# A graph network on one core: other association of the products, transposes laid on the host, and the stages of two pairs alternating

## The chip, the cores and the metric

The kernel runs on one core of a Trainium2 chip, all in float32. The metric is the device time of one launch in microseconds (us). The profile names the engines PE (TensorE matmul), PEld (TensorE weight load), DVE (VectorE), ACT (ScalarE), POOL (GpSimd) and SP (the queue that issues the loads).

## The reference, cut to what matters

There are 64 graphs of N = 256 nodes with D = 512 features, and a dense adjacency of 256 x 256 each.

```python
# layer 0: three graph convolutions, each  adj @ (h @ W) + b
h = relu(adj @ (x @ W1) + b1)
h = relu(adj @ (h @ W2) + b2)
x = layernorm(x + adj @ (h @ W3) + b3)
# layer 1: one weight per node, softmax over a graph's nodes
q, k = split(x @ Wqk, 2); v = x @ Wv
w = mask / sqrt(D) * rowsum(q * (adj @ (mask * k)))
x = layernorm(x + softmax(w)[:, None] * v)
```

## The kernel before: the parts that matter here

It works on 32 pairs of graphs. A layer is made as (adj @ h) @ W: the aggregation comes out transposed, features on partitions, and so serves as the stationary operand of the projection. The scores are rowsum((x1 @ M) * (adj @ (mask * x1))) with M = Wq @ Wk.T.

```python
def transpose_adj(i, aj, k):                       # 4 TensorE transposes a graph
    pt = psum.tile([P, NH, N], FP, name="pa", tag="mm")
    for m in range(NH):
        for h in range(NH):
            nc.tensor.transpose(pt[:, m, h * P:(h + 1) * P], aj[:, k, h, m * P:(m + 1) * P], ident)
    aT = work.tile([P, NH, N], FP, name="aT", bufs=4)
    nc.scalar.copy(aT, pt)
    ...                                            # aTm = aT * mask, on GpSimd

# aggregate(h, aT):     16 products of 128x256 per pair  -> pz
# project(srcT, w, h):  16 products of 128x512 per pair  -> pp

for i in range(NP + 1):
    ...
    aTs = [transpose_adj(i, aj, k) for k in ks]
    if last is not None:
        sm = softmax_rows(last[2])
    zs = [aggregate(xt[:, k], aTs[k][0]) for k in ks]
    ...
    if last is not None:                           # layer 1's end, one pair late
        s = softmax_cols(sm)
        for k in ks:
            layer1_out(i - 1, k, last[0][k], last[1][k], s)
    for n in range(2):
        hs = [hidden(zs[k], n) for k in ks]        # VectorE adds the bias, ScalarE does Relu
        zs = [aggregate(hs[k], aTs[k][0]) for k in ks]
    x1s = [layer0_out(zs[k], xt[:, k]) for k in ks]
    x1Ts = [scores(i, k, x1s[k], aTs[k][1], w) for k in ks]
```

Of the kernel before, what the change touches and what calls it, by code (L numbers as in the profile page):

```python
# [13 lines left out]


@with_exitstack
def gcn_then_graph_attention(ctx: ExitStack, tc: tile.TileContext, x, adj, nodemask,
                             W1, b1, W2, b2, W3, b3, Wqk, Wv, out):
    """Layer 0: x1 = LN(x + GCN3(x)), each GCN layer as (adj @ h) @ W + b.
    Layer 1: x2 = LN(x1 + softmax_i(w) * (x1 @ Wv)), with  # L20
    w = mask / sqrt(D) * rowsum((x1 @ (Wq @ Wk.T)) * (adj @ (mask * x1))).

    adj @ h is made transposed (features on partitions), which is the form that
    the product with W takes as its stationary operand; that product comes out
    with nodes on partitions again. Two graphs go side by side, so that the
    tensor engine has one's products while the other's are brought out of PSUM.
    """
    nc = tc.nc
    P = 128
    B, N, D = x.shape  # L30
    NH = N // P
    DC = D // P
    PAIR = 2
# [5 lines left out]
    work = ctx.enter_context(tc.tile_pool(name="work", bufs=2))  # L39
# [4 lines left out]
    def load_pair(i):  # L44
        bs = slice(i * PAIR, (i + 1) * PAIR)
        aj = loads.tile([P, PAIR, NH, N], FP, name="aj")
        nc.sync.dma_start(aj, adj[bs].rearrange("b (h p) m -> p b h m", p=P))
        xt = loads.tile([P, PAIR, NH, D], FP, name="xt")
        nc.sync.dma_start(xt, x[bs].rearrange("b (h p) f -> p b h f", p=P))  # L49
        return xt, aj  # L50
# [6 lines left out]
    loaded = load_pair(0)  # L57

    mask_n = const.tile([B, N], FP, name="mask_n")
    nc.sync.dma_start(mask_n, nodemask)  # L60

    def load_w(w, name):
        t = const.tile([P, DC, D], FP, name=name)
        nc.sync.dma_start(t, w.rearrange("(c p) h -> p c h", p=P))
        return t

    def load_b(b, name):
        t = const.tile([P, D], FP, name=name)
        nc.sync.dma_start(t, b.partition_broadcast(P))
        return t  # L70

    wl, bl = [], []
    for n, (w, b) in enumerate(((W1, b1), (W2, b2), (W3, b3))):
        wl.append(load_w(w, f"w{n}"))
        bl.append(load_b(b, f"b{n}"))
    wqk_rows = []
    for f in range(DC):
        t = work.tile([P, 2 * D], FP, name="wqk", tag="x1", bufs=4)
        nc.sync.dma_start(t, Wqk[f * P:(f + 1) * P, :])
        wqk_rows.append(t)  # L80
    wv = load_w(Wv, "wv")

    mask_t = const.tile([P, NH, B], FP, name="mask_t")
    mask_s = const.tile([P, NH, B], FP, name="mask_s")
    pm = psum_s.tile([P, NH, B], FP, name="pm", tag="sm")
    for h in range(NH):
        nc.tensor.transpose(pm[:, h, :], mask_n[:, h * P:(h + 1) * P], ident[:B, :B])
    nc.vector.tensor_copy(mask_t, pm)
    nc.vector.tensor_scalar(mask_s, mask_t, ISCALE, None, op0=OP.mult)

    m_qk = const.tile([P, DC, D], FP, name="m_qk")

    def make_m():
        """m_qk = Wq @ Wk.T"""
        halves = []
        for s in range(2):
            for dp in range(DC // 2):
                t = work.tile([P, 2, D], FP, name="wqkT", tag="x1T", bufs=4)
                for k in range(2):
                    c = s * D + (2 * dp + k) * P  # L100
                    pt = psum.tile([P, D], FP, name="pt", tag="mm")
                    for f in range(DC):
                        nc.tensor.transpose(pt[:, f * P:(f + 1) * P], wqk_rows[f][:, c:c + P], ident)  # L103
                    if k:
                        nc.vector.tensor_copy(t[:, k, :], pt)
                    else:
                        nc.scalar.copy(t[:, k, :], pt)
                halves.append(t)
        qT, kT = halves[:DC // 2], halves[DC // 2:]
        for f in range(DC):  # L110
            pt = psum.tile([P, D], FP, name="pt", tag="mm")
            for d in range(DC):
                nc.tensor.matmul(pt, lhsT=qT[d // 2][:, d % 2, f * P:(f + 1) * P], rhs=kT[d // 2][:, d % 2, :],  # L113
                                 start=(d == 0), stop=(d == DC - 1))
            nc.scalar.copy(m_qk[:, f, :], pt)

    def transpose_adj(i, aj, k):
        pt = psum.tile([P, NH, N], FP, name="pa", tag="mm")
        for m in range(NH):
            for h in range(NH):  # L120
                nc.tensor.transpose(pt[:, m, h * P:(h + 1) * P], aj[:, k, h, m * P:(m + 1) * P], ident)  # L121
        aT = work.tile([P, NH, N], FP, name="aT", bufs=4)
        nc.scalar.copy(aT, pt)  # L123
        aTm = work.tile([P, NH, N], FP, name="aTm", bufs=4)
        b = i * PAIR + k
        for m in range(NH):
            nc.gpsimd.tensor_scalar(aTm[:, m, :], aT[:, m, :], mask_t[:, m, b:b + 1], None, op0=OP.mult)  # L127
        return aT, aTm

    def aggregate(h_in, aT):  # L130
        """(adj @ h).T, features on partitions"""
        zT = work.tile([P, DC, N], FP, name="zT", bufs=3)
        for fp in range(DC // 2):
            pz = psum.tile([P, 2, N], FP, name="pz", tag="mm")
            for j in range(2):
                f = 2 * fp + j
                for m in range(NH):
                    nc.tensor.matmul(pz[:, j, :], lhsT=h_in[:, m, f * P:(f + 1) * P], rhs=aT[:, m, :],  # L138
                                     start=(m == 0), stop=(m == NH - 1))
            if fp % 2:  # L140
                nc.vector.tensor_copy(zT[:, 2 * fp:2 * fp + 2, :], pz)  # L141
            else:
                nc.scalar.copy(zT[:, 2 * fp:2 * fp + 2, :], pz)  # L143
        return zT

    def project(srcT, w, h):
        """rows of half h of src @ w, from src transposed"""
        pp = psum.tile([P, D], FP, name="pp", tag="mm")
        for f in range(DC):
            nc.tensor.matmul(pp, lhsT=srcT[:, f, h * P:(h + 1) * P], rhs=w[:, f, :],  # L150
                             start=(f == 0), stop=(f == DC - 1))
        return pp

    def hidden(zT, n):
        hn = work.tile([P, NH, D], FP, name="hn", bufs=3)
        for h in range(NH):
            pp = project(zT, wl[n], h)
            t = work.tile([P, D], FP, name="t", bufs=3)
            nc.vector.tensor_tensor(t, pp, bl[n], op=OP.add)  # L159
            nc.scalar.activation(hn[:, h, :], t, AF.Relu)  # L160
        return hn

    def layernorm(dst, src):
        st = small.tile([P, NH, 6], FP, name="st")
        mv = small.tile([P, NH, 2], FP, name="mv")
        for h in range(NH):
            nc.vector.bn_stats(st[:, h, :], src[:, h, :])  # L167
            nc.vector.bn_aggr(mv[:, h, :], st[:, h, :])  # L168
        sd = small.tile([P, NH], FP, name="sd")
        nc.scalar.activation(sd, mv[:, :, 1], AF.Sqrt, bias=eps)  # L170
        rs = small.tile([P, NH], FP, name="rs")
        nc.vector.reciprocal(rs, sd)
        for h in range(NH):
            nc.vector.tensor_scalar(dst[:, h, :], src[:, h, :], mv[:, h, 0:1], rs[:, h:h + 1],  # L174
                                    op0=OP.subtract, op1=OP.mult)

    def layer0_out(zT, xb):
        r = work.tile([P, NH, D], FP, name="r", bufs=2)
        for h in range(NH):
            pp = project(zT, wl[2], h)  # L180
            nc.vector.tensor_tensor(r[:, h, :], pp, xb[:, h, :], op=OP.add)  # L181
        x1 = work.tile([P, NH, D], FP, name="x1", bufs=4)
        layernorm(x1, r)
        return x1

    def transpose_x1(x1):
        x1T = work.tile([P, DC, N], FP, name="x1T", bufs=4)
        for fp in range(DC // 2):
            pt = psum.tile([P, 2, N], FP, name="px", tag="mm")
            for j in range(2):  # L190
                f = 2 * fp + j
                for h in range(NH):
                    nc.tensor.transpose(pt[:, j, h * P:(h + 1) * P], x1[:, h, f * P:(f + 1) * P], ident)  # L193
# [26 lines left out]
    def softmax_rows(w):  # L220
        """softmax over the nodes, one graph per partition"""
        pw = psum_s.tile([PAIR, N], FP, name="pw", tag="sm")
        for h in range(NH):
            nc.tensor.transpose(pw[:, h * P:(h + 1) * P], w[:, h, :], ident)  # L224
# [32 lines left out]
    for i in range(NP + 1):  # L257
# [16 lines left out]
        if i == NP:  # L274
            break
# [32 lines left out]
```

## Time and profile before

| | before |
|---|---|
| time, median of 2 runs | 3232.23 us |
| span of the profiled run | 3230.6 us |
| TensorE busy | 3215.3 us (100%) |
| VectorE, ScalarE, GpSimd busy | 32%, 17%, 9% |
| TensorE starts / last product ends | 8.12 / 3223.4 us |
| one pair in mid-run | 99.85 us |
| granted TensorE clock | 0.999 |

The chain of work that ended last is followed back from the last instruction, each step to what released it. TensorE has it from 8.12 us until the last product. What comes after is short. These are the last pieces of that chain in order of time (start, length in us, what; a bare "issue" is time in which nothing that the profile shows was waited for):

```profile
3213.79 9.65 PE pp L150 x22
...
3223.47 0.76 DVE r L248
3224.25 0.70 DVE st L167
...
3226.28 0.46 DVEq L304
```

Only 7.2 us follow the last product (3223.44 to 3230.6): VectorE needs few instructions for the last half graph, and the output is written graph by graph. One more line belongs here, from the groups of waits (engine and what it was about to do, on whom it waited, us in total, times, longest):

```profile
PEld pz L138 <- ACT aT L123: 5.6, 31, 0.2
```

Once in each pair, the weight load of the first aggregation waits for the copy of the transposed adjacency.

### The profile page before, as it was taken

The numbers are of one execution on the slowest core, as the hardware profiler recorded it, in microseconds if no ns is written. First come the engines' busy times: TensorE is split into PE (matmuls) and PEld (weight loads), VectorE is DVE, ScalarE is ACT, GpSimd is POOL, SyncE is SP. The second block draws the span as 40 slices with busy tenths as digits, with TensorE's granted clock in tenths as the row PEclk, the third lists the DMA queues.
The fourth block names the chain that finished last, engine by engine and source line by source line (L and its number), as shares of the span: only waits on it lengthen the run. The fifth ranks groups of instructions, "written<-read, shape, count | busy, mean of one in ns | idle before, by whom it ended". The sixth has DMA issues, their size and how long they took to land.

```text
span 3230.6 us, 23926 instructions
## 1 busy us (share of the span) xinstructions
PE 3215.3 (100%) x9666; PEld 1753.3 (54%) x9666; DVE 1033.9 (32%) x2055; ACT 561.7 (17%) x970; POOL 276.0 (9%) x262
## 2 busy tenths in 40 slices
PE   8999999999999999999999999999999999999999
PEld 5555555555555555555555555555555555555554
DVE  1332323323333233233332332323323333333233
ACT  2111111111111111111111111111111111111111
POOL 1110011110111101111001110011110111101110
PEclk9999999999999999999999999999999999999999
DMA  3110001000000000010000000001000001000000
GB/s 134 33 33 20 26 20 33 33 20 26 20 33 33 20 26 21 32 33 26 26 27 20 33 30 23 26 20 33 33 20 26 20 33 33 20 26 20 26 14 13
DMA packets 54509, 92.55 MB, mean 29 GB/s; under 512 B 2240, under 2 KB 18688, under 8 KB 54400
## 3 DMA queue, kind: packets, MB, share of 16 engines
q1 hardware_dynamic: 54400, 91.04, 8.3%
q8 instruction: 76, 1.25, 0.2%
q14 instruction: 33, 0.27, 0.0%
HBM read 57.48 MB, written 33.55 MB: 28 GB/s over the span
## 4 chain that ended last, share of the span: by engine, by line
PE 100%; DMA 0%; DVE 0%; SPq 0%; DVEq 0%; issue 0%; ACT 0%
PE pp L150 68%; PE pz L138 21%; PE pg L208 7%; PE px L193 2%; PE pa L121 1%; PE pt L113 0%; PE pw L224 0%; PE ps L239 0%; DMA mask_n<-in_nodemask 0%; PE pt L103 0%; DVE r L248 0%; DVE st L167 0%; DVE o L174 0%; SPq L49 0%; DVEq L304 0%
## 5 line engine op out<-in xcount | busy, mean ns | idle before, releaser
L150 PE MATMUL pp<-w,zT 128*128 128x512 f32 x3072 | 1334.0, 592 | 0.0
L150 PEld LDWEIGHTS pp<-w,zT 128*128 128x128 f32 x3072 | 583.7, 190 | 707.4 <-issue 704.1
L138 PE MATMUL pz<-aT,hn 128*128 128x256 f32 x2048 | 452.5, 379 | 0.0
L150 PE MATMUL pp<-m_qk,x1T 128*128 128x512 f32 x1024 | 449.9, 592 | 0.0
L150 PE MATMUL pp<-wv,x1T 128*128 128x512 f32 x1024 | 448.3, 595 | 0.0
L138 PEld LDWEIGHTS pz<-aT,hn 128*128 128x128 f32 x2048 | 389.1, 190 | 80.2 <-issue 30.6
L159 DVE TENSOR_TENSOR t<-pp,b 128x512 f32<-128x512 f32 x256 | 177.1, 692 | 626.5 <-PE pp L150 626.5
L127 POOL TENSOR_SCALAR aTm<-aT,mask_t 128x256 f32<-128x256 f32 x128 | 117.0, 932 | 2817.8 <-ACT aT L123 2817.8
L150 PEld LDWEIGHTS pp<-m_qk,x1T 128*128 128x128 f32 x1024 | 194.6, 190 | 244.9 <-issue 244.9
L150 PEld LDWEIGHTS pp<-wv,x1T 128*128 128x128 f32 x1024 | 191.8, 190 | 229.5 <-issue 229.0
L160 ACT ACTIVATE hn<-t 128x512 f32<-128x512 f32 x256 | 161.3, 630 | 782.0 <-DVE t L159 782.0
L141 DVE COPY zT<-pz 128x512 f32<-128x512 f32 x192 | 132.9, 692 | 470.2 <-PE pz L138 470.2
L216 DVE SCALAR_TENSOR_TENSOR prod<-pp,mask_s,g 128x512 f32<-128x512 f32 x128 | 96.1, 751 | 499.2 <-PE pp L150 499.2
L138 PE MATMUL pz<-aT,xt 128*128 128x256 f32 x1024 | 231.3, 384 | 0.0
L208 PE MATMUL pg<-x,aTm 128*128 128x512 f32 x512 | 230.3, 592 | 0.0
L138 PEld LDWEIGHTS pz<-aT,xt 128*128 128x128 f32 x1024 | 193.2, 191 | 31.0 <-ACT aT L123 5.6
L170 ACT ACTIVATE sd<-mv,eps 128x2 f32<-128x2 f32 x128 | 37.9, 296 | 836.8 <-DVE mv L168 836.8
L167 DVE BATCH_NORM_STATS2 st<-r 128x6 f32<-128x512 f32 x256 | 177.5, 693 | 7.7
L248 DVE SCALAR_TENSOR_TENSOR r<-pp,s,x 128x512 f32<-128x512 f32 x128 | 96.1, 751 | 219.4 <-PE pp L150 219.4
L143 ACT COPY zT<-pz 128x512 f32<-128x512 f32 x192 | 111.6, 581 | 296.2 <-PE pz L138 296.2
L269 POOL TENSOR_TENSOR xt<-xt,b 128x512 f32<-128x512 f32 x128 | 159.3, 1264 | 25.1 <-PE pz L138 20.4
L181 DVE TENSOR_TENSOR r<-pp,xt 128x512 f32<-128x512 f32 x128 | 88.5, 692 | 227.5 <-PE pp L150 218.9
(45 smaller groups left out, 893.2 us busy)
## 6 DMA issues: line engine op xcount, KB each, us to landing
xt<-in_x SPq DMA_DIRECT2D x32, 1024.0 KB, 5.4
out<-o SPq DMA_DIRECT2D x64, 512.0 KB, 2.8
aj<-in_adj SPq DMA_DIRECT2D x32, 512.0 KB, 3.8
w<-in_L_gnn_W SPq DMA_DIRECT2D x3, 1024.0 KB, 10.6
wqk<-in_L_gnn_Wqk SPq DMA_DIRECT2D x4, 512.0 KB, 11.9
wv<-in_L_gnn_Wv SPq DMA_DIRECT2D x1, 1024.0 KB, 12.3
b<-in_L_gnn_b SPq DMA_DIRECT2D x3, 256.0 KB, 11.1
mask_n<-in_nodemask SPq DMA_DIRECT2D x1, 64.0 KB, 6.2
```

What stands on the lines that cost most here:

```text
L127: nc.gpsimd.tensor_scalar(aTm[:, m, :], aT[:, m, :], mask_t[:, m, b:b + 1], None, op0=OP.mult)
L138: nc.tensor.matmul(pz[:, j, :], lhsT=h_in[:, m, f * P:(f + 1) * P], rhs=aT[:, m, :], start=(m == 0), stop=(m == NH - 1))
L141: nc.vector.tensor_copy(zT[:, 2 * fp:2 * fp + 2, :], pz)
L143: nc.scalar.copy(zT[:, 2 * fp:2 * fp + 2, :], pz)
L150: nc.tensor.matmul(pp, lhsT=srcT[:, f, h * P:(h + 1) * P], rhs=w[:, f, :], start=(f == 0), stop=(f == DC - 1))
L159: nc.vector.tensor_tensor(t, pp, bl[n], op=OP.add)
L160: nc.scalar.activation(hn[:, h, :], t, AF.Relu)
L167: nc.vector.bn_stats(st[:, h, :], src[:, h, :])
L208: nc.tensor.matmul(pg, lhsT=aTm[:, m, h * P:(h + 1) * P], rhs=x1[:, m, :], start=(m == 0), stop=(m == NH - 1))
L216: nc.vector.scalar_tensor_tensor(prod, py, mask_s[:, h, b:b + 1], gs[h], op0=OP.mult, op1=OP.mult, accum_out=w[:, h, k:k + 1])
L248: nc.vector.scalar_tensor_tensor(r[:, h, :], pv, s[:, h, k:k + 1], x1[:, h, :], op0=OP.mult, op1=OP.add)
L269: nc.gpsimd.tensor_tensor(xt[:, k, h, :], xt[:, k, h, :], bl[2], op=OP.add)
```

## The change

Its intent is to take all transposes but that of x1 off TensorE, to fold the hidden layers' biases into the eviction, and to keep TensorE supplied by giving it another pair's stage between any two stages of one pair. A layer becomes adj @ (h @ W), the scores become masked-adj * (y @ x1.T) with y = x1 @ M, and x and adj come in twice, natural and transposed by the host. The core of the diff (loads, weight layouts and signature are cut):

```diff
-        aT = work.tile([P, NH, N], FP, name="aT", bufs=4)
-        nc.scalar.copy(aT, pt)                        # and the transposes into pt
+    def load_aT(i):
+        t = loads.tile([P, G, NH, N], FP, name="aT", bufs=3)
+        nc.sync.dma_start(t, adjT[i])
 ...
-            t = work.tile([P, D], FP, name="t", bufs=3)
-            nc.vector.tensor_tensor(t, pp, bl[n], op=OP.add)
-            nc.scalar.activation(hn[:, h, :], t, AF.Relu)
+            nc.scalar.activation(hT[:, f], pz, AF.Relu, bias=bias[:, f:f + 1])
 ...
-            pg = psum.tile([P, D], FP, name="pg", tag="mm")         # adj @ (mask x1), 128x512
-            py = project(x1T, m_qk, h)                              # x1 @ M
+            pg = psum.tile([P, NH, N], FP, name="pg", tag="mm")     # y @ x1.T, 128x256
+            for h in range(NH):
+                for d in range(DC):
+                    nc.tensor.matmul(pg[:, h, :], lhsT=yT[:, d, g, h * P:(h + 1) * P], rhs=x1T[:, d, g, :],
+                                     start=(d == 0), stop=(d == DC - 1))
 ...
+    for i in range(NP + 1):
+        new = i < NP
+        if new:              s = project(x0, w1, "s", 2)
+        if prev is not None: layer0_out(prev, aTs[i - 1], xt)
+        if new:              hT = aggregate_relu(s, aTs[i], bl1)
+        if prev is not None: x1T = transpose_x1(xt)
+        if new:              s = project(hT, w2, "s", 2)
+        if prev is not None: yT = project_T(x1T, wm)
+        if new:              hT = aggregate_relu(s, aTs[i], bl2)
+        if prev is not None: w = scores(i - 1, yT, x1T, an)
+        if new:              s = project(hT, w3, "s", 2)
+        if prev is not None:
+            sm = softmax_rows(w)
+            v = project(x1T, wv, "vs", 1)
+            layer1_out(i - 1, xt, v, softmax_cols(sm))
```

## The prediction

> **What bounds the kernel now.** I read first the page's busy time by engine, then its chain of work that ended last, then the same chain in order of time over one pair of graphs in mid-run, and last the groups of waits.
>
> ```profile
> PE 3215.3 (100%) x9666; PEld 1753.3 (54%) x9666; DVE 1033.9 (32%) x2055; ACT 561.7 (17%) x970; POOL 276.0 (9%) x262
> ...
> PE 100%; DMA 0%; DVE 0%; SPq 0%; DVEq 0%; issue 0%; ACT 0%
> ```
>
> TensorE is busy for 3215.3 of 3230.6 us, and the chain is TensorE from beginning to end: no eviction, no load and no semaphore is on it except at the two ends. A busy TensorE could still be a stretched one, so I look at one period of the chain, from one start of a layer-1 projection to the next (1055.46 to 1155.31, 99.85 us for a pair):
>
> ```profile
> 1055.46 13.73 PE pp L150 x32
> 1069.19 6.91 PE pz L138 x32
> 1076.10 13.73 PE pp L150 x32
> 1089.83 0.87 PE px L193 x8
> ...
> 1112.18 0.88 PE pa L121 x8
> 1113.06 0.30 PE pw L224 x2
> 1113.36 7.16 PE pz L138 x32
> 1120.52 0.21 PE ps L239 x2
> 1120.73 27.66 PE pp L150 x64
> 1148.40 6.91 PE pz L138 x32
> ```
>
> The columns are start, length, what. One program matmul of 128x512 leaves two records; 32 records last 13.73 us, so such a matmul costs 0.858 us, one of 128x256 0.432 us (6.91 / 16), a 128x128 transpose 0.109 us (0.87 / 8). These are start-to-start rates, not the longer means of the page's groups, which contain the drain.
>
> **What the Trainium skill says.** "FP8 and Floating Point Precision", section TensorE Precision Notes, gives true FP32 four passes through the array. "TensorE: Matmul & The Clock Gate", section Back-to-back issue gap, gives 518 cycles for one pass of 512 columns at 2.4 GHz, 0.216 us. Four make 0.863 us; this trace has 0.858, so it agrees, and the two kernels cannot differ in rate as long as the type stays. "PSUM — Partial Sum Buffer", section The four PSUM rules, limits one matmul output to one 2 KiB bank, so the seven general buffers of either kernel hold seven stages' outputs of 128x512 in flight. "DMA: Bandwidth & Descriptors", section Anatomy of one DMA, fits about 2.0 us plus bytes over 436 GB/s for a transfer on another issuing path; here 1 MB of x takes 5.4 us (median of 32), somewhat slower than that fit's 4.4.
>
> **The change part by part.** TensorE first, since only it matters. Counting the loops per pair before: three layers of 16 projections, 8 for adj @ x1, 16 with m_qk and 16 with Wv make 88 matmuls of width 512; three aggregations of 16 make 48 of width 256; 8 adjacency and 16 x1 transposes. After: 3 x 16 projections, 8 for the third layer's adj @ s, 16 for y = x1 @ M and 16 with Wv: again 88. Two aggregations of 16 and 16 for y @ x1.T: again 48. So associating the product the other way, and taking the scores from y @ x1.T, **trades equal for equal**: an N x N product over D costs what the removed third aggregation cost. What goes is the transposing.
> - Removed per pair: 8 transposes, 0.88 us; over 32 pairs 28 us. Also the first aggregation's wait for their copy: it took 7.16 instead of 6.91 us, about 0.2 us each, and the groups of waits agree: weight loads of pz waited for the copy to aT 31 times, up to 0.2 us. That is 6 to 8 us. At start-up, 32 transposes of Wqk (3.7 us) and two of the mask (0.4 us). Sum: **38 to 40 us removed**, 1.2% of the time, all of it on the path.
> - Removed elsewhere: bias additions as separate VectorE work (256 x 692 ns = 177 us) become part of the Relu eviction; copies of the transposed adjacency (34.5 us of ScalarE) and its masking. VectorE had 68% idle, ScalarE 83%: this is worth nothing. Plain copies of the projections (8 a pair with Wv's) come in; estimated from rows of the page, VectorE's work per pair is 14 copies or adds at 0.69, 8 statistics at 0.69 and 8 aggregations at 0.18, 8 normalizations at 0.54, 4 scale-and-adds at 0.75, 4 products over 256 columns at about 0.45: some 27 us in a period of 99.
> - Added traffic: x and adj come twice, once transposed: about 4.3 MB a pair with the output, against 2.5, so 43 GB/s where start-up shows 370 to 410 in stretches of 2 to 4 us. The issue order has each load of a pair almost one period ahead. Hidden.
> - Moved: the third layer's end and all of layer 1 of pair i-1 now lie between the stages of pair i. In the built order each consumer in TensorE's queue has a whole stage of the other pair before it. The tightest is normalization: with layer-0 output starting at 0, its products end at 6.9 and the aggregation of the other pair at 13.7; VectorE needs add 0.69, statistics 0.69 + 0.18, square root 0.36 with its semaphore, reciprocal 0.17, two normalizations 1.1 after the last product, so about 10.7 with one Relu before the square root. Then 3 us of slack. The stages of the fill (pair 0 alone) need the last eviction, about 0.97 us after the last product, only after three 0.43 us matmuls of other operands: no stall either.
> So a full iteration is five stages of 13.73 (W1, W2, W3, M, Wv), two aggregations of 6.91, 6.87 for layer 0's output, 6.91 for scores, 1.75 for transposes and 0.51 for the small ones: 98.5. I take 98.65 for small interruptions.
> - Start: the first matmul now needs x transposed and all of W1, 2 MB. Before, 1.56 MB had landed at 7.98 us (the wait for the mask, at the chain's head); at 380 GB/s another 0.5 MB is 1.3 us: TensorE starts at about 9.3 instead of 8.1. The first few microseconds ran slower before as well (first pz stage 8.72 for 7.16): 1.7 us.
> - **End**: the last pair has no partner. From the end of the previous pair's Wv: VectorE finishes that pair's output (about 8.9 us of work), then adds and normalizes the last pair; its rows in the built order sum to 18.9 us until the second graph is normalized; a transpose and a copy later, at about 20.2, y can begin. TensorE has 8.6 us of work in that time, so 11 to 12 us are idle. Then 13.73 + 6.91 + 13.73 + 0.8 of products: 55.4. Then copies, scale-and-add and normalization of four half-graphs, 9.6 us, and a 1 MB write of about 5.5 us (0.5 MB took 3.9 to the end of the span before): 70.5, and 1.7 for a slower restart. Of 72 us TensorE works 44; so 28 idle against 7.2 after the last product before: **21 us added**.
>
> Sum from below: 9.3 + 1.7 + fill 68.7 (four stages of 13.73, two of 6.91) + 31 x 98.65 = 3058.2 + 72.2 gives a span of 3210.1; the timed run was 1.6 longer than the span: 3211.7. By differences: 3232.2 - 39 + 1.2 + 21 = 3215.4. I take 3213.
>
> **The rivals.**
> - The alternation stalls each pair: single buffers for hT, x1T, yT and the projected values could make TensorE wait. For it: the pools are shallower, and VectorE does layer 1's output beside the next projection. Against: every writer of those follows its last reader by a stage of 7 to 14 us, and a buffer of PSUM is asked back seven allocations later. Missing by 2 us would give about 3275; it takes 2.7 us a period to be slower by 2%.
> - The end costs less, because the scheduler's rows overlap better or the write is hidden: 3200. Or more, with the span near 3222.
> - A larger win, as the intent suggests: no adjacency transposes, biases inside the evictions, TensorE never waiting. Against: TensorE's remaining products alone are 2832 x 0.858 + 1536 x 0.432 + 512 x 0.109 + 16 = 3166 us; a gain over 2% would need 3168. All but impossible.
> - Loads in the loop arriving late (xT has a single buffer). Its load can go out when the first projection ends, 85 us ahead: no.
>
> **Range and chances.** The removal is sure within 3 us, the end within 8, the period within 0.3 (9 us over 31). Range 3203 to 3226. Faster by over 2%: 0.01. Within 2%: 0.97. Slower: 0.02, for a stall in each period that I missed.
>
> **What would show it.** The chain of the changed kernel should again be nearly all TensorE, in periods of 98.5 to 98.9 us, without a row for adjacency transposes; 2832 x 2 records of width 512 and 1536 x 2 of width 256. The timeline of the last 72 us should show a gap of about 11 us before the last pair's y, and VectorE, ScalarE and the write after the last product. Wrong would be: waits of TensorE for ScalarE or VectorE counted 31 times at over a microsecond, a matmul of width 512 that is not 0.858 us, or a first product much after 9.3 us.

## The result

The changed kernel takes 3205.21 us (median of 2 runs, 3205.07 to 3205.35); the ratio to the kernel before is 0.9917, with a 95% interval of 0.9898 to 0.9936, which counts as the same, since a difference under 2% is not called faster or slower here. A ratio here is the mean time of one kernel's fast runs over that of the other's fast runs of the same rounds, so it is not quite the ratio of the medians quoted. From the page of the changed kernel, the busy times and the chain:

```profile
PE 3175.8 (99%) x9376; PEld 1723.1 (54%) x9376; DVE 858.3 (27%) x1858; ACT 564.8 (18%) x966; POOL 225.0 (7%) x102
...
PE 99%; DVE 1%; DMA 0%; issue 0%; DVEq 0%; SPq 0%; ACT 0%
```

TensorE is still nearly the whole chain, with 39.5 us less busy time; VectorE has lost 176 us of work, of which nothing shows in the time (the last experiment tests that). One period of the chain, from one softmax transpose to the next:

```profile
1051.68 13.73 PE pw L83 x32
1065.41 0.21 PE ps L190 x2
1065.62 13.93 PE pw L83 x32
1079.55 6.87 PE pp L138 x16
1086.42 6.91 PE pz L114 x32
1093.33 1.75 PE px L151 x16
...
1108.81 13.73 PE py L97 x32
1122.54 6.91 PE pz L114 x32
1129.45 6.91 PE pg L162 x32
1136.36 13.73 PE pw L83 x32
1150.09 0.22 PE pw L175 x2
```

The period is 98.63 us (1051.68 to the end of the last line, 1150.31), against 99.85. Each stage follows the former without a gap, and each lasts what its number of products costs (one has 0.2 us more). There is no line for an adjacency transpose, and the first aggregation takes 6.91 us where it took 7.16. What speaks against the change is at the end. TensorE's timeline there (start, length, engine, line, operation, with the idle time before it in brackets):

```profile
3136.82 7.13 PE L138 MATMUL pp<-s,aT 128*128 128x512 f32 x16
3149.83 1.95 PE L151 MATMUL px<-ident,xt 128*128 128x128 f32 x8 [5.88 <-issue]
3152.23 2.00 PE L151 MATMUL px<-ident,xt 128*128 128x128 f32 x8 [0.45 <-DVE xt L130]
3154.26 15.09 PE L97 MATMUL py<-x1T,wm 128*128 128x512 f32 x32
...
3190.15 0.29 PE L190 MATMUL ps<-ident,smx 2*128 2x2 f32 x2
```

The last pair has no partner. Between its layer-0 products and its transposes TensorE idles 5.88 us while VectorE finishes the former pair and normalizes this one, and what follows runs slowly: the transposes, then 15.09 us for the stage that takes 13.73. The granted clock reads 0.50 from 3149.8 to 3154.2 us and 0.70 from there to 3158. After the last product, at 3190.4, another 13.2 us pass, where it was 7.2 us before.

### The profile page after: what moved, and what is told of

Its sections match the earlier page's. It is cut to its first block, busy times and chain, and to the rows that moved or that the text cites. A ratio compares the mean times of both kernels' runs of the same rounds, so it can differ in the third digit from the quotient of the medians.

```text
span 3203.6 us, 22542 instructions
## 1 busy us (share of the span) xinstructions
PE 3175.8 (99%) x9376; PEld 1723.1 (54%) x9376; DVE 858.3 (27%) x1858; ACT 564.8 (18%) x966; POOL 225.0 (7%) x102
## 4 chain that ended last, share of the span: by engine, by line
PE 99%; DVE 1%; DMA 0%; issue 0%; DVEq 0%; SPq 0%; ACT 0%
PE pw L83 55%; PE pz L114 14%; PE py L97 14%; PE pg L162 7%; PE pp L138 7%; PE px L151 2%; PE pt L239 0%; DVE st L123 0%; PE pw L175 0%; DMA w<-in_W 0%; PE ps L190 0%; DVE xt L198 0%; DVE xt L130 0%; DVE xt L140 0%; DVE vs L86 0%; DVE mv L124 0%
## 5 line engine op out<-in xcount | busy, mean ns | idle before, releaser
L83 PE MATMUL pw<-w,hT 128*128 128x512 f32 x2048 | 889.4, 592 | 0.0
L83 PEld LDWEIGHTS pw<-w,hT 128*128 128x128 f32 x2048 | 386.7, 190 | 460.9 <-issue 436.9
L83 PE MATMUL pw<-w,xT 128*128 128x512 f32 x1024 | 450.1, 598 | 8.3 <-DMA w<-in_W 8.3
L114 PE MATMUL pz<-aT,s 128*128 128x256 f32 x2048 | 452.5, 379 | 0.0
L97 PE MATMUL py<-x1T,wm 128*128 128x512 f32 x1024 | 445.9, 593 | 0.0
L83 PE MATMUL pw<-wv,x1T 128*128 128x512 f32 x1024 | 445.0, 592 | 0.0
L114 PEld LDWEIGHTS pz<-aT,s 128*128 128x128 f32 x2048 | 389.1, 190 | 80.2 <-issue 30.6
L97 PEld LDWEIGHTS py<-x1T,wm 128*128 128x128 f32 x1024 | 195.0, 191 | 245.5 <-issue 245.0
L162 PE MATMUL pg<-x1T,yT 128*128 128x256 f32 x1024 | 226.2, 379 | 0.0
L138 PE MATMUL pp<-s,aT 128*128 128x512 f32 x512 | 225.1, 592 | 0.0
```

Of the source, the lines that this page charges most:

```text
L83: nc.tensor.matmul(pp, lhsT=hT[:, f, g, h * P:(h + 1) * P], rhs=w[:, f, :], start=(f == 0), stop=(f == DC - 1))
L97: nc.tensor.matmul(pp, lhsT=w[:, f, o * P:(o + 1) * P], rhs=hT[:, f], start=(f == 0), stop=(f == DC - 1))
L114: nc.tensor.matmul(pz[:, g, :], lhsT=s[:, g, m, f * P:(f + 1) * P], rhs=aT[:, g, m, :], start=(m == 0), stop=(m == NH - 1))
L138: nc.tensor.matmul(pp, lhsT=aT[:, g, m, h * P:(h + 1) * P], rhs=s[:, g, m, :], start=(m == 0), stop=(m == NH - 1))
L162: nc.tensor.matmul(pg[:, h, :], lhsT=yT[:, d, g, h * P:(h + 1) * P], rhs=x1T[:, d, g, :], start=(d == 0), stop=(d == DC - 1))
```

## The experiments

All eight kernels gave correct results. They ran in two calls of four; the kernel before was 3232.29 us in the first and 3231.74 us in the second (medians of 9 runs each). The medians of the experiments are of 4 or 5 runs.

### The kernel before, adjacency transposed by the host

```diff
-        nc.sync.dma_start(aj, adj[bs].rearrange("b (h p) m -> p b h m", p=P))
+        nc.sync.dma_start(aj, adj[i])                 # laid transposed on the host
 ...
-                nc.tensor.transpose(pt[:, m, h * P:(h + 1) * P], aj[:, k, h, m * P:(m + 1) * P], ident)
-        nc.scalar.copy(aT, pt)
+        aT = aj[:, k]
```

> The kernel before, with the adjacency laid transposed on the host and its 256 TensorE transposes taken out; nothing else changed. Theory (the gain per pair is the transposes and the wait for their copy, all on TensorE's path): 3232.2 - 27.9 (32 x 0.87) - 7.6 (the first aggregation back from 7.16 to 6.91 us, 31 times) = about 3197 us, which is faster than the changed kernel, since it has not that kernel's long end. Rival (the gain comes from the new association of the products and the alternation): 3225 to 3232 us.

Measured: 3196.6 us, ratio 0.9890 (0.9876 to 0.9903). This one part of the change, in the old kernel, gives more than the whole change. In the chain in order of time, the first aggregation is back to plain work, interrupted only by the softmax transposes:

```profile
1100.24 0.11 PE pw L219
1100.35 0.87 PE pz L133 x4
1101.21 0.20 PE pw L219
1101.41 6.05 PE pz L133 x28
```

(0.87 + 6.05 = 6.92.) The period, from the third aggregation at 1057.24 to the next at 1155.98, is 98.74 us: 1.11 less than before, the 0.87 of the transposes and 0.24 of the wait.

### The changed kernel, adjacency transposed on TensorE again

```diff
             s = project(x0, w1, "s", 2)
+            aTs[i] = transpose_adj(aTs[i])            # 8 transposes, copied by ScalarE
```

> The changed kernel with the adjacency transposed on TensorE again, after the first projection, where its copy has time. Theory: 32 x 0.87 = 28 us more than 3205.2, so 3233 us, about level with the kernel before: the rest of the change is then worth nothing or a little less. Rival (the gain comes from the rest of the change): under 3212 us.

Measured: 3235.07 us, ratio 1.0009 (0.9996 to 1.0021). The chain has this line back in each period:

```profile
1089.47 0.87 PE pa L62 x8
```

Without the host's transposes the rest of the change is, as a whole, worth nothing. With the two kernels themselves this makes a table of two by two:

| | transposes on TensorE | by the host | difference |
|---|---|---|---|
| old order of products | 3232.3 | 3196.6 | -35.7 |
| new order, alternating | 3235.1 | 3205.2 | -29.9 |
| difference | +2.8 | +8.6 | |

The old kernel gains 27.9 us for the transposes and 7.4 for the wait for their copy (0.24 us times 31 pairs). In the new one a stage of other work hides that wait. Its 29.9 is 2 us more than the transposes alone: pair 0 has no other pair beside it and waits 0.7 us for the copy, its first aggregation takes 7.17 us, and y after the gap at the end takes 16.06 instead of 15.09.

The last row is not the order of products alone: it contains the new kernel's long end, which two experiments below remove (9.0 and 6.7 us).

### The changed kernel, scores as before

```diff
-            yT = project_T(x1T, wm)
+            w, gs = scores(i - 1, xt, x1T, aTm)       # g = adj @ (mask x1), 8 products of 128x512
 ...
-            w = scores(i - 1, yT, x1T, an)
+            w = scores_end(i - 1, x1T, w, gs)         # x1 @ M, 16 of 128x512; rowsum with g
```

> The changed kernel with scores as before: g = adj @ (mask x1) and y = x1 @ M, both 128x512, and the row sum of their product. Theory: 24 products of 0.858 us per pair against 16 of 0.858 and 16 of 0.432, equal to 0.04 us, so 3200 to 3210 us, with more VectorE and ScalarE work that is hidden. Rival (the scores from y @ x1.T save time on the path): above 3220 us.

Measured: 3202.82 us, ratio 0.9911 (0.9895 to 0.9926). The form of the scores is neutral within the interval. Some 3 us of span are gained (3200.4 against 3203.6): the period is 98.60 instead of 98.63, and in the trace's last stretch g, which needs no transpose, follows the transposes at once, so that y has its usual 13.73 us. The gap of 5.88 us and the slow transposes are there too, but g takes its usual 6.87 us: the granted clock, 0.50 to 0.53 during the transposes, reads 1.00 from 3152.3 us on, where g begins. How long the low clock lasts after a gap thus differs between two kernels with the same gap; why is open.

### The changed kernel, without alternation

```diff
+    for i in range(NP):                               # all stages of pair i in a row
+        s = project(x0, w1, "s", 2)
+        ...
+        s = project(hT, w3, "s", 2)
+        layer0_out(s, aTs[i], xt)
+        x1T = transpose_x1(xt)
+        yT = project_T(x1T, wm)
```

> The changed kernel with each pair's stages one after the other, no second pair between them. Theory (the alternation hides each stage's eviction): TensorE waits per pair for the last graph's normalization (about 2.5 us), for the copy of its transpose (about 0.9) and for the score products (0.5 to 1), so 4 to 5 us a pair and up to 1.4 more for a slower restart: 3320 to 3380 us. Rival (seven PSUM buffers and the order of instructions hide these anyway): about 3190 us, as the long end is then gone.

Measured: 3367.75 us, ratio 1.0420 (1.0406 to 1.0434); the mean granted clock over the span fell to 0.976. TensorE's timeline at one normalization in mid-run, then the table of stretches for the same place (the number after POOL's busy time is the granted clock):

```profile
1011.80 7.03 PE L138 MATMUL pp<-s,aT 128*128 128x512 f32 x16
1019.12 1.29 PE L151 MATMUL px<-ident,xt 128*128 128x128 f32 x8 [0.29 <-issue]
1022.22 1.85 PE L151 MATMUL px<-ident,xt 128*128 128x128 f32 x8 [1.81 <-DVE xt L130]
1024.11 15.06 PE L97 MATMUL py<-x1T,wm 128*128 128x512 f32 x32
```

```profile
1019.00:1022.30 3.30, 1.37 (x9) 0.93 (x10) 2.83 (x9) 1.27 (x3) 0.00 (x0) 1.00 0.51 159
1022.30:1024.20 1.90, 1.85 (x9) 1.21 (x9) 0.32 (x1) 0.68 (x2) 0.00 (x0) 0.65 0.00 0
1024.20:1028.00 3.80, 3.80 (x7) 1.80 (x8) 0.00 (x0) 0.49 (x1) 0.00 (x0) 0.73 0.00 0
```

The waits themselves are small, 0.29 and 1.81 us here, 67.8 us for this line in the whole run. As large is what comes with the lower granted clock after them. The busy time of y, without alternation and in the changed kernel:

```profile
L97 PE MATMUL py<-x1T,wm 128*128 128x512 f32 x1024 | 495.0, 645 | 2.0 <-ACT x1T L152 1.0
```

```profile
L97 PE MATMUL py<-x1T,wm 128*128 128x512 f32 x1024 | 445.9, 593 | 0.0
```

The transposes take 100.6 us instead of 63.2. So the alternation hides 160 us of span (3363.7 - 3203.6), net of the long end that it brings. But it is not a gain over the kernel before, which hid the same with the two graphs of one pair.

### The end: a partner for the last pair

```diff
             layer0_out(prev, aTs[i - 1], xt)
+            if not new:                               # held: the last pair but one
+                v = project(held[1], wv, "vs", 1)
+                layer1_out(i - 2, held[0], v, softmax_cols(held[2]))
```

> The changed kernel; only at the end, the Wv projection of the last pair but one is put behind the layer-0 output of the last pair. In the changed kernel's trace the stretch from the end of the last pair's layer-0 products (3143.75) to the end of its y (3169.36) is 25.6 us for 15.5 us of TensorE work. Theory (the extra length of the end is this missing partner): about 9 of those 10 us go, 3196 us. Rival (VectorE's total work at the end sets it): under 3 us go, since the same work is only moved.

Measured: 3196.24 us, ratio 0.9889 (0.9876 to 0.9903). The same part of TensorE's timeline:

```profile
3122.51 7.03 PE L138 MATMUL pp<-s,aT 128*128 128x512 f32 x16
3129.38 13.90 PE L83 MATMUL pw<-wv,x1T 128*128 128x512 f32 x32
3143.21 0.28 PE L190 MATMUL ps<-ident,smx 2*128 2x2 f32 x2
3143.42 1.97 PE L151 MATMUL px<-ident,xt 128*128 128x128 f32 x16
3145.78 14.00 PE L97 MATMUL py<-x1T,wm 128*128 128x512 f32 x32 [0.40 <-ACT x1T L152]
```

The gap of 5.88 us is down to 0.40, and y is at full speed again. VectorE's work is the same in sum; only what TensorE has to do meanwhile was moved. The rival falls.

### The end: output per graph, out of PSUM

```diff
-            v = project(x1T, wv, "vs", 1)
-            layer1_out(i - 1, xt, v, softmax_cols(sm))
+                last_out(i - 1, xt, x1T, sm)          # last pair: as the kernel before does it
```

> The former, and the last pair's output taken per graph straight out of PSUM and written per graph. Theory: the drain after the last product falls from 13.2 to the 7.2 us of the kernel before: 6 us off, 3190 us. Rival (the write of 1 MB is what takes the time, split or not): 2 us or less.

Measured: 3189.53 us, ratio 0.9869 (0.9856 to 0.9883). In the chain, VectorE's part after the last product (at 3180.47) is this, and the span ends at 3187.6, 7.1 us later:

```profile
3173.39 7.08 PE pl L212 x16
...
3180.49 0.76 DVE xt L218
3181.27 0.70 DVE st L123
...
3183.35 0.46 DVEq L342
```

Both parts of the end were sized about right: 9.0 us (9 expected) and 6.7 (6 expected). The second run changes two things at once, the copies out of PSUM and the split write; the traces divide the drain between them. Against the run before, VectorE's part after the last product falls from 7.9 to 2.9 us, and what follows it until the end of the span from 5.4 to 4.3: most of the gain is VectorE's.

### The start: first loads in four pieces

```diff
-    x0 = load_xT(0)
-    w1 = load_w(W1, "w1")
+    for f in range(DC):
+        nc.sync.dma_start(x0[:, f], xT[0][:, f])
+        nc.sync.dma_start(w1[:, f], W1[:, f])
```

> The former, and the first 2 MB of loads (x transposed and W1) split into four pieces by chunk of features, so that TensorE can begin after the first 0.5 MB. Theory: the first product begins at about 5 instead of 8.3 us and data keeps ahead: 3 us off, 3187 us. Rival (the pieces land together, or the slow first microseconds take as much): no gain.

Measured: 3187.07 us, ratio 0.9862 (0.9847 to 0.9877). The head of the chain in the changed kernel, and in this one:

```profile
1.18 6.94 DMA w<-in_W
8.12 0.14 issue
8.26 16.23 PE pw L83 x32
```

```profile
1.18 4.29 DMA w<-in_W
5.47 0.14 issue
5.61 15.75 PE pw L83 x32
```

TensorE starts 2.65 us earlier and its first stage is no slower. The intervals of this kernel and the one above overlap, but each of its four runs (3186.66 to 3187.93) is faster than each of the other's (3189.37 to 3190.47), and the chain shows where. This version has the shortest time of all that ran, 1.4% under the kernel before.

### The bias back on VectorE

```diff
-            nc.scalar.activation(hT[:, f], pz, AF.Relu, bias=bias[:, f:f + 1])
+            nc.vector.tensor_scalar(t, pz, bias[:, f:f + 1], None, op0=OP.add)
+            nc.scalar.activation(hT[:, f], t, AF.Relu)
```

> The changed kernel with the bias of the two hidden layers added by VectorE in an operation of its own ahead of the Relu, as in the kernel before: 256 operations of 0.69 us, 177 us more of VectorE work. Theory (VectorE's load is not on the path): 3203 to 3208 us. Rival (taking work off VectorE is part of the gain): some 3210 us or more.

Measured: 3207.36 us, ratio 0.9922 (0.9909 to 0.9934), level with 0.9917. VectorE's busy time is 1030.9 us instead of 858.3, and the period is again 98.63 us (in its trace 1051.27 to 1149.90). The 172 us are hidden. The span is 1.9 us longer, partly in the end, where y took 15.66 us after the gap instead of 15.09; a difference of this size is within the scatter of the runs.

## Why the prediction was right

- **The bound.** TensorE carries 99% of the chain (100% before); no wait of a microsecond recurs. Right. One side remark was not: seven PSUM buffers hold seven outputs of 128x512, not seven stages', since a stage of 13.73 us writes four. Nothing in the sum rested on it.
- **Equal for equal.** Right. Both pages have the 5664 records of width 512 (592 to 598 ns on average in a group) and 3072 of width 256 (379 to 384) that were counted. With the adjacency transposed by the host in both kernels, a period's projections take 68.86 us in both, and its stages of 128x256 take 20.74 (old) and 20.73 us (new). The scores' form moves the time by less than its interval.
- **Removed.** 38 to 40 us predicted. The period fell by 1.22, and 31 times that is 37.8 us. TensorE's busy time fell by 39.5, but it also contains the slow stages at the start and at the end, so this closeness is partly chance. The removal was then tested by itself: 35.7 us in the old kernel, where 35.5 was expected.
- **The period.** 98.65 predicted, 98.63 measured.
- **VectorE, ScalarE, traffic.** Right: VectorE has 26.64 us of work in a period (27 estimated, by luck so close: some 1.4 us of it are the slow normalization of the next point), and putting 172 us back changes nothing that the runs resolve.
- **Normalization's slack.** Three us were reckoned. In the trace it ended at 1091.58 and the transposes began at 1093.33, so 1.75 were left: one normalization took 1.9 us instead of 0.54, which the working did not have (see the last section). It was enough.
- **The start.** 9.3 us was 8.26, so the first 2 MB came faster than estimated; the slow first stage cost 2.5 us and not 1.7. These almost cancel.
- **The end.** 72.2 us predicted, 66.8 measured (3136.8 to 3203.6). The kind of each loss was right, and each was shown by taking it away, but the length was 5.4 us too large. The term was VectorE's rows, which I summed with their full lengths. In the trace they overlap: two statistics take 1.28 us and not 1.39, the pairs of normalizations 1.0 and not 1.09, an aggregation that another operation follows adds 0.08 or 0.09 to the chain and not 0.18. All these rows took 15.9 us (3136.7 to 3152.6) where 18.9 had been put, and y began 17.4 us after the former pair's end and not 20.2. The drain took 13.2 us from the last product, where 9.6 + 5.5 = 15.1 had been put.

Added up: -1.0 at the start, +0.8 in its speed, -0.6 in the periods, -5.4 at the end is -6.2; the span reckoned from below was 3210.1 and came out at 3203.6. The figure on record (3213) lay above that sum, as it leaned towards the sum by differences (3215.4), which carried the same error of the end. The time, 3205.2, is 2 us above the lower end of the range: the second rival, an end that costs less because VectorE's rows overlap (3200), came true in good part.

Where the intended gain went is thus shown: the host's transposes give 36 us in the old kernel; the new order of products gives nothing in the period, since TensorE has the same products to do; and the alternation across pairs, which must be paid for by a last pair without a partner, gives back part of it. With that end repaired the time is 3189.5, and with the start, 3187.1. The repaired 3189.5 is some 7 us under the old kernel with the host's transposes (3196.6). By the traces about 3.4 of them lie in the period (98.74 against 98.63, 31 times, mostly the softmax transposes' place) and about 4 in the transposes of Wqk and the mask, which the old kernel still makes at its start; no run separates these.

The 2.5 us that the first stage loses lie in its first six records: they take 5.1 us, about 0.85 each instead of 0.43, and then the rate is the usual one. That is half speed, but the granted clock reads 1.00 there, so the cause is not shown. Not separated by any run is also what the new order of products would give with the two graphs of one pair alternating, as in the old kernel.

## What to carry to other kernels

When one engine has the whole chain, count its work on both sides of the change before all else: a reordering that trades products for products, and relief of engines that idle, are worth nothing, while each small instruction taken off that engine is worth its full start-to-start time. A pipeline across successive items hides waits in the middle and shows them at the end; hold back one independent stage of the item before as a partner for the last one. A pause of TensorE can cost more than its length: where only transposes and waits lay between two stages of products (5.3 us without alternation, 10.5 at the changed kernel's end), the granted clock fell to between 0.50 and 0.73 for some microseconds. With the gap filled (0.40 us left) it stayed at 1.00.

## What the Trainium skill lacked or had wrong

- "TensorE: Matmul & The Clock Gate", section LDWEIGHTS (loading the stationary operand), puts a weight load of 128 columns at 128 / 1.2 = 107 ns, without regard to type. It lacks the record of a float32 load: 190 ns (2048 loads for the hidden layers' projections), and 143 ns for those of the transposes. This does not refute the page, since a record is not a spacing: the 16 loads for the transposes of a pair took 1.88 us together (from 1092.95), 117 ns each.
- The same page's table of cycles (section Back-to-back issue gap) has no float32 row. The runs show, start to start, 0.858 us for 128x512 (two records of 0.429), 0.432 us for 128x256 and 0.109 us for a 128x128 transpose; a transpose's record is 273 ns long, near the 275 ns that the page's Part 4 (PE-mode transpose) has from one kernel's context, but back to back it is the 109 ns that count.
- "SBUF — State Buffer", section Who interferes with whom, says that VectorE in a two-port mode and GpSimd block each other for a whole instruction. The runs agree, as far as they go: while GpSimd's 4.51 us addition ran (from 1083.21), a pair of normalizations took 2.39 instead of 1.0 us, and single ones took up to 4.11 us in the changed kernel. Without alternation the addition falls elsewhere, and none of the 256 normalizations took over 0.55 us. The page has no case of a layer normalization; that it runs in such a mode no view shows.
- "TensorE: Matmul & The Clock Gate", section Why this matters for your kernels, advises no idle gaps over about 3 us between bursts of matmuls, which reads as if waits of 0.29 and 1.81 us were harmless. Without alternation they lay around eight transposes and were followed by a granted clock of 0.65 and 0.73, and by 15.06 us for y, which takes 13.9 in that view. The advice is not wrong, if transposes are left out of the count, for the page's Part 4 says that they don't count as busy in the same way: from the end of the products to y 5.3 us passed. What the table lacks is that word about transposes. No run put other work in their place.
